# Layer 1's moves, a mixing, the last values, a plan and the short blocks take other places in the order of a two-layer attention kernel

## The chip, the core and the metric

The kernel runs on one core of a Trainium2 chip. The core has TensorE (PE: matrix products into the eight banks of PSUM), VectorE (DVE), ScalarE (ACT), GpSimd (POOL) and SyncE (SP), which here issues DMAs. The engines run at the same time. Each works through its own list of instructions in order, and they wait for one another through semaphores. The metric is the time of one execution on the device in microseconds (us); a change is judged by the median of several executions.

## What is computed

The input has 8 images of 256 channels and 32 x 32 = 1024 positions, all in 32-bit floats. Layer 0 is attention with 8 heads of 64. Layer 1 is attention with one head of 256 on normed tokens, then a mixture of 8 experts, 2 for each token:

```python
# layer 0: 8 heads, softmax over the queries (axis 1)
qkv = (xt @ w_qkv + b_qkv).reshape(B, S, N_HEADS, 3 * D_K)
attn = softmax(einsum('bihd,bjhd->bijh', q, k) * SCALE, axis=1)
x = einsum('bijh,bjhd->bihd', attn, v) @ w_out + b_out + xt
# layer 1: attention and experts, each on normed tokens, each added to t
n = layer_norm(t); scores = (n @ W.T) @ n.T
t = t + softmax(scores) @ n
n = layer_norm(t)
probs = softmax(n @ router_w.T); rw, re = top_k(probs, 2); rw = rw / rw.sum()
out = n
for e in range(8):
    h = gelu(n @ w1[e] + b1[e])
    out = out + combine[:, e:e + 1] * (h @ w2[e] + b2[e])
t = t + out
```

## The kernel before

**Order.** The kernel is written as a straight program. A planner sorts the instructions of each engine: it goes by the order in which they were written and by when its own model of costs says that their inputs are ready, so a later instruction that is ready passes an earlier one that is not. `tc.issue_after(x)` adds an edge: what is written inside comes after `x` on `x`'s own engine, and only there. Tiles have a fixed number of buffers; an instruction that writes one waits until its last reader is done. In PSUM there are three tiles of two banks ("big") and two of one bank ("acc"). A 32-bit product of 512 columns stands in the trace as two instructions.

**Images.** Images 0 to 6 run layer 0 (`layer0`), layer 1's attention (`attend`), the norm (`normed`) and the routing (`dispatch`), which scatters each token's row to the place of its expert in memory. Image 7 runs its layer 0, then the experts of the 7 other images (`experts`), then its own attention, and then the experts of its own tokens densely (`dense`), while the other images' results are added up and stored.

**Layer 0.** For each of 4 pairs of heads (g) there are 8 steps (j). Step `at` makes scores for the two heads (L531, two halves of 512 queries each), their maxima in two halves (L546, L555), the exps (L572), and, two steps later, the product with the values (`po`, L608). The values are divided by the exps' sums first (`vs`, L588). Eight blocks of values are projected ahead of the step that needs them: six during the image before, and the last two by `begun.rest()` after step 0 (L414, with additions L436 on DVE). The pairs' queries and keys are projected at the steps in `PROJECT`: (0, 3), (1, 1) and (2, 1) (`pqk`, L384); at the first of these the routing of the image before goes on, with two small products in a free bank (L1141) and a copy of them (L1147). At the last of these, DVE transposes the image into tokens (`residual`, L483), and in the two steps after it POOL adds the output's bias (L490). After 32 steps the heads are projected out (`pr`, L716). Between `po`'s two parts stand empty instructions on SP (`relay`, L618).

**The plan.** In image 7, `plan` computes which block of tokens belongs to which expert: a first part on DVE at step (1, 1), a second at (2, 1), before `residual` there. The last six small operations of the second part make three tables of addresses (L1310, L1313).

**Layer 1's attention.** Scores are made by a scheme with 7 products in place of 8, for four pairs of token blocks (`Pair`). `open` copies the first product (L797, ACT), starts the z product in an acc bank (L819) and adds (L829, DVE); `middle` makes a second copy (L808); `end` a third (L814); `rest` finishes, with the maxima and exps (L857 to L875). Each block's exps are then turned: a DVE transpose (L896) and 16 moves of 32 x 256, 8 by ACT and 8 by SP's DMAs (L908). `mix` multiplies them with the tokens (`py`, L925, an acc bank) and adds the result to the tokens on DVE (L934), which frees the bank. The order of these calls is written out by hand at the end of `attend`.

**Experts.** The rows of the 7 images are cut into 63 blocks: 56 full ones of 256 tokens and 7 short ones of 128, in an order that `Group` sets. For each block ACT copies the expert's weights into a ring (L1366), SP fetches rows (L1382), DVE transposes them (L1395), PE makes two layers of products (L1406, L1435), ACT the gelu (L1418), DVE adds the bias and multiplies by the gate (L1445, L1459), and POOL scatters the rows by indirect DMAs (L1466). The last 4 blocks (`LATE`) finish during image 7's attention.

**Dense.** For image 7, POOL adds the normed tokens (L1120) after the transposes of `normed`; DVE computes the gates (L1020 to L1606). Then, for each expert and half, PE makes `pdh` (L1630) and `pdy` (L1654), ACT the gelu (L1639) and DVE the weighted sum (L1664). At the third of the 16 rounds `biases` transposes the gates (L1612), copies them (L1614, ACT), multiplies them with the biases (`pb`, L1618) and adds (L1621).

Of the kernel before, what the change touches and what calls it, by code (L numbers as in the profile page):

```python
# [19 lines left out]
def kernel(  # L20
# [23 lines left out]
    nc = tc.nc  # L44
    P = 128
# [5 lines left out]
    NCC = C // P  # L51
# [443 lines left out]
    def layer0(b, xT, begun, routing, xs):  # L495
# [148 lines left out]
        for at in range(last + LAG + 1):  # L644
# [15 lines left out]
            if at <= last:  # L660

                with tc.issue_after(seconds[1].ins) if 1 in seconds else nullcontext():
                    first_max(at, 0)
                score(at, 0, 1)
                score(at, 1, 0)
                second_max(at, 0)
                if not early:
                    soften(at, 0)
                with tc.issue_after(seconds[0].ins):
                    ahead = divide(at - 1) if at > 0 else seconds[0]  # L670
                    if parts and at > 0:
                        parts.pop(0)(ahead)
                with tc.issue_after(ahead.ins):
                    first_max(at, 1)
            elif at == last + 1:
                evicted["divided"] = divide(last)
            if at == 0:
                score(0, 1, 1)
                second_max(0, 1)
                soften(0, 1)  # L680
                begun.rest()
                share()
# [5 lines left out]
            if at <= last and (g, j) in PROJECT:  # L688
                with tc.issue_after(firsts[at, 1].ins), tc.issue_after(array.ins):
                    share(firsts[at, 1])  # L690
                    pair, pq, mm = project_pair(b, xT, g + 1)
                qks.append(pair)
                if (g, j) == PROJECT[-1]:
                    ahead = firsts[at, 1]
                    if b == B - 1:
                        with tc.issue_after(ahead.ins):
                            ahead = next(planning)
                    with tc.issue_after(ahead.ins):
                        t1, parts = residual(b, xs)
                if g == 0:  # L700
                    with tc.issue_after(mm.ins), tc.issue_after(firsts[at, 1].ins):
                        counted = share(pq)
                if b == B - 1 and (g, j) == PROJECT[1]:
                    planning = plan(groups[0])
                    with tc.issue_after(firsts[at, 1].ins):
                        next(planning)
            elif at <= last and (g, j) > PROJECT[1]:
                share(firsts[at, 1])
        for _ in routing:
            pass  # L710
# [12 lines left out]
    def attend(b, t1, fill, tick=nothing, n1=None):  # L723
# [54 lines left out]
        class Pair:  # L778
# [17 lines left out]
            def open(self):  # L796
                self.first = nc.scalar.copy(self.left, self.x)  # L797
                if self.k < 3:
                    second = self.product(self.v, a12, b21, True)
                    tc.declare_no_dep(second.ins, self.first.ins, reason="the other bank")  # L800
                self.z = acc(f"ps1z_{b}_{self.k}")
                self.product(self.z, s1_, t1_, True)
                self.add(self.left, self.v, 3.0e38, self.low[0])
# [116 lines left out]
        def mix(at, aT, ssum, more):  # L920
# [16 lines left out]
            tick(("mixed", at), mixed)  # L937

# [23 lines left out]
        third = turned(*third, (pairs[2].first, pairs[2].second))  # L962
        fourth = turned(*fourth, (pairs[2].second, pairs[2].second))
        mix(*second)
        fifth, sixth = pairs[2].rest()
        pairs[3].open()
# [91 lines left out]
    class Group:  # L1058


        def __init__(self, n, items):
# [5 lines left out]
            halves = [(2 * j + 1) * self.nb // (2 * self.half) for j in range(self.half)]  # L1067
# [29 lines left out]
    def normed(b, t2, fill, tick=nothing, norm=None):  # L1097
# [16 lines left out]
        else:  # L1114
            with tc.issue_after(copied.ins):
                fill("turned")
            for part, at in ((n2.first, slice(0, NT - 1)), (n2.last, slice(NT - 1, NT))):
                for cc in range(NCC):
                    some = t2[:, at].rearrange("p i (k cc c) -> p cc i k c", k=NQ, c=SQ)[:, cc]
                    added = nc.gpsimd.tensor_add(  # L1120
                        some, some, part[:, :, ts(cc, P)].rearrange("p i (k c) -> p i k c", c=SQ)
                    )
                    tc.add_manual_dep(added.ins, evicted["scaled"].ins.name, BEHIND)
# [88 lines left out]
    def plan(group):  # L1212
# [94 lines left out]
        placed = nc.vector.tensor_copy(row_at[:, :nb], lo)  # L1307
        where = [row_at]
        for what, each in (("w", WE), ("b1", NFC), ("b2", D)):
# [4 lines left out]
            where.append(at)  # L1314
        group.where = where
        yield placed
# [271 lines left out]
    def dense(b, t2, norm, fill, begin, table):  # L1588
# [3 lines left out]
        _, nT, l = normed(b, t2, fill, norm=norm)  # L1592
# [13 lines left out]
        nc.vector.tensor_add(all_gates, all_gates, second)  # L1606

        def biases():

            pg = big(f"pg_{b}")  # L1610
            for i in range(NT):
                nc.tensor.transpose(pg[:E, ts(i, P)], all_gates[:, i, :], ident)  # L1612
            gT = two.tile([E, S], F32, tag="tr", name=f"gT_{b}")
            nc.scalar.copy(gT, pg[:E, :])  # L1614
            for i in range(0, NT, 2):
                pb = acc(f"pb_{b}_{i}")
                for j in range(2):
                    nc.tensor.matmul(  # L1618
                        pb[:, ts(j, D)], gT[:, ts(i + j, P)], b2_rows, start=True, stop=True
                    )  # L1620
# [63 lines left out]
        for at, (e, n) in enumerate((e, n) for e in range(E) for n in range(NH2)):  # L1684
            hT, mm = hidden(e, n, collected)
            if at == 2:
                biases()
            if pending is not None:
                collected = collect(*pending, mm)
            pending = e, n, hT  # L1690
# [106 lines left out]
```

## Time and profile before

| what | us |
|---|---|
| median of 3 runs (2270.83 to 2273.49) | 2272.08 |
| the profiled execution, its own time | 2274.83 |
| its span, first to last instruction | 2273.1 |
| busy of TensorE's weight loads (beside the products) | 1200.3 |
| scores of layer 0 (L531), busy | 566.0 |
| values product of layer 0 (L608), busy | 568.5 |
| exps of layer 0 (L572), busy on ACT | 570.4 |
| layer 0 of an image, first scores to the first output product (image 6: 1461.1 to 1602.7) | 141.6 |
| the same for image 7 (1700.2 to 1848.0) | 147.8 |
| experts of 7 images (1862.0 to 2062.4) | 200.4 |

In lists of the trace a line gives the start and the length in us, the engine, the line of the kernel, the operation, the tiles (what is written, an arrow, what is read), the shape and how many were merged. In brackets stands how long the engine had been idle before, and what ended that. "PEld" are weight loads, "SPq" is SyncE's queue. In tables by window the first entries are the stretch and its length, then for each engine its busy time and count, then the granted clock of TensorE (1.00 is full), the DMA engines' busy share and GB/s. Granted clock over the whole run: 0.996.

### The profile page before, as it was taken

What the parts mean: (1) busy time and instruction counts of PE and PEld (TensorE: products, weight loads), DVE (VectorE), ACT (ScalarE), POOL (GpSimd) and SP (SyncE); (2) the same over time, 40 slices, a digit from 0 to 9 for tenths busy, and PEclk for the clock granted to TensorE, in tenths of its full rate; (3) what the DMA queues carried; (4) which work ended last, traced back from release to release, by engine and by line L of the source; (5) the groups of instructions that cost most, each with busy time, mean ns of one, the idle gap of its engine ahead of it and who ended that gap; (6) DMA issues with size and microseconds to landing.
All of it is one profiled execution on the core that took longest, in us unless ns stands there. A gap on an engine that the chain in (4) does not pass through costs nothing.

```text
span 2273.1 us, 38013 instructions
## 1 busy us (share of the span) xinstructions
PE 2231.4 (98%) x13033; PEld 1200.3 (53%) x13033; DVE 1567.1 (69%) x3924; ACT 1231.3 (54%) x2221; POOL 309.7 (14%) x327
## 2 busy tenths in 40 slices
PE   9999999999999999999999999999999999999998
PEld 3345534563356335543555345534563368885666
DVE  5775678567865787577756775678557857665667
ACT  3664566356636564746554664566355655555411
POOL 1000012000300030002000120002000315551100
PEclk9999999999999999999999999999999999999999
DMA  8996201020102010111011010200032036662485
GB/s 279 357 352 199 53 15 43 3 61 7 51 1 46 19 51 7 31 35 43 15 19 46 20 38 10 55 13 27 1 78 64 31 70 148 149 148 48 120 276 169
DMA packets 273449, 181.89 MB, mean 80 GB/s; under 512 B 191860, under 2 KB 228519, under 8 KB 272232
## 3 DMA queue, kind: packets, MB, share of 16 engines
q1 hardware_dynamic: 260328, 149.16, 24.3%
q0 software_dynamic: 11296, 29.78, 3.6%
q8 instruction: 104, 1.70, 0.3%
q14 instruction: 89, 0.73, 0.1%
q10 hardware_dynamic: 1632, 0.52, 0.1%
HBM read 62.55 MB, written 105.70 MB: 74 GB/s over the span
## 4 chain that ended last, share of the span: by engine, by line
PE 80%; issue 5%; ACT 4%; DVE 4%; SPq 2%; POOL 2%; DMA 1%; POOLq 0%; DVEq 0%; ACTq 0%
PE po L608 20%; PE psc L531 20%; PE pqk L384 7%; PE py L925 7%; PE pr L716 5%; PE pv L414 4%; PE ps L819 3%; PE px L756 2%; POOL y L1466 2%; SPq L908 2%; PE pdh L1630 2%; PE pdy L1654 2%; PE pqk L362 2%; PE ps1z L819 2%; PE ph L1406 1%
## 5 line engine op out<-in xcount | busy, mean ns | idle before, releaser
L572 ACT ACTIVATE ex<-psc,nmax 128x1024 f32<-128x1024 f32 x512 | 570.4, 1115 | 298.8 <-DVE scrap L555 215.6
L608 PE MATMUL po<-ex,vs 64*64 64x512 f32 x4096 | 568.5, 592 | 5.3 <-DVE vs L588 4.3
L531 PE MATMUL psc<-qk,qk 64*64 64x512 f32 x4096 | 566.0, 593 | 3.7 <-ACT ex L572 3.6
L555 DVE TENSOR_SCALAR_CACHE_REDUCE scrap<-psc,nmax 128x512 f32<-128x512 f32 x512 | 384.5, 751 | 158.5 <-PE psc L531 129.8
L546 DVE TENSOR_REDUCE nmax<-psc 128x1 f32<-128x512 f32 x512 | 350.8, 685 | 10.7 <-PE psc L531 10.7
L531 PEld LDWEIGHTS psc<-qk,qk 64*64 64x64 f32 x4096 | 178.0, 132 | 275.1 <-ACT ex L572 129.0
L608 PEld LDWEIGHTS po<-ex,vs 64*64 64x64 f32 x4096 | 172.9, 132 | 284.0 <-DVE vs L588 87.6
L1203 POOL DMA_INDIRECT rows<-n,d_at x112 | 109.2, 975 | 463.4 <-DVE nmax L546 425.1
L384 PE MATMUL pqk<-xT,wqkv 128*128 128x512 f32 x384 | 171.2, 599 | 0.0
L1466 POOL DMA_INDIRECT y<-yb,to x119 | 117.4, 986 | 209.2 <-DVE yb L1459 185.6
L349 ACT ACTIVATE qk<-pqk,b_qks 128x512 f32<-128x512 f32 x124 | 85.6, 690 | 88.8 <-PE pqk L384 79.7
L384 PEld LDWEIGHTS pqk<-xT,wqkv 128*128 128x128 f32 x384 | 71.0, 190 | 99.9 <-issue 77.3
L908 ACT COPY spare<-home 32x256 f32<-32x256 f32 x272 | 109.4, 402 | 17.3 <-DVE home L896 11.9
L414 PE MATMUL pv<-wqkv,xT 128*128 128x512 f32 x244 | 116.4, 600 | 1.0 <-DVE v L436 1.0
L925 PE MATMUL py<-n,spare 128*128 128x256 f32 x512 | 114.9, 379 | 0.0
L1195 POOL IOTA n<- 128x8 f32 x14 | 2.0, 145 | 820.5 <-PE py L925 820.5
L1406 PE MATMUL ph<-xb,w_ring 128*128 128x256 f32 (+1 forms) x488 | 110.7, 370 | 2.9 <-DVE xb L1395 2.8
L716 PE MATMUL pr<-wo,res 128*128 128x256 f32 x512 | 111.9, 379 | 0.7 <-ACT res L627 0.7
L925 PEld LDWEIGHTS py<-n,spare 128*128 128x128 f32 x512 | 96.4, 190 | 20.1 <-issue 4.3
L716 PEld LDWEIGHTS pr<-wo,res 128*128 128x128 f32 x512 | 97.2, 190 | 17.8 <-ACT res L627 4.7
L1418 ACT ACTIVATE hb<-ph,b1T 128x256 f32<-128x256 f32 (+1 forms) x126 | 51.3, 459 | 101.1 <-PE ph L1406 101.1
L1435 PE MATMUL pe<-w_ring,hb 128*128 128x256 f32 x444 | 105.5, 379 | 0.0
(265 smaller groups left out, 2836.8 us busy)
## 6 DMA issues: line engine op xcount, KB each, us to landing
rows<-zero SPq DMA_DIRECT2D x7, 8256.0 KB, 62.4
xr<-rows SPq DMA_DIRECT2D x224, 64.0 KB, 2.0
xs<-in_x_dram SPq DMA_DIRECT2D x64, 128.0 KB, 3.9
ys<-y SPq DMA_DIRECT2D x16, 512.0 KB, 6.4
spare<-home SPq DMA_DIRECT2D x240, 32.0 KB, 1.9
out_dram<-oT SPq DMA_DIRECT2D x58, 128.0 KB, 3.8
xT<-in_x_dram SPq DMA_DIRECT2D x7, 1024.0 KB
sums<-t SPq DMA_DIRECT2D x7, 1024.0 KB
```

The lines of the kernel that those rows point to most:

```text
L384: mm = nc.tensor.matmul(pq[:, ts(n, 512)], wqkv[:, cc, t, ts(g, P)], xT[:, cc, ts(n, 512)], start=(cc == 0), stop=(cc == NCC - 1),)
L414: return nc.tensor.matmul(pv, self.xT[:, cc, ts(i, P)], wqkv[:, cc, 2, :], start=(cc == 0), stop=(cc == NCC - 1),)
L531: mm = nc.tensor.matmul(pss[at, h][ts(c, DK), ts(n, 512)], k[r, j * P + c * DK : j * P + (c + 1) * DK], q[r, ts(n, 512)], start=True, stop ...
L546: firsts[at, h] = nc.vector.tensor_reduce(nmax, pss[at, h][:, ts(0, 512)], AX.X, ALU.max, negate=True)
L555: seconds[h] = nc.vector.tensor_scalar(scrap, pss[at, h][:, ts(1, 512)], -1.0, nmaxes[at, h], ALU.mult, ALU.min, accum_out=nmax,)
L572: nc.scalar.activation(ex, pss.pop((at, h)), AF.Exp, bias=nmaxes.pop((at, h)), scale=1.0, accum_out=sums[at][:, h : h + 1],)
L608: mm = nc.tensor.matmul(po[n][ts(h, DK), :], vss[at][keys, h, :], exps[at, h][keys, ts(n, 512)], start=(j == 0 and turn == 0), stop=(j == ...
L716: nc.tensor.matmul(pr[:, :C], res[g][:, ts(i, P)], wo[:, g, :], start=(g == 0), stop=(g == NPAIR - 1))
L908: move(to[ts(k, SQ), a], since[ts(a, SQ), k])
L925: evicted["mixed"] = nc.tensor.matmul(py[:, :D], aT[m], n1[:, m, :], start=(m == 0), stop=(m == NT - 1))
L1406: last = nc.tensor.matmul(ph[:, ts(fc, br)], wb[:, dc * FF + fc * P : dc * FF + (fc + 1) * P], xb[:, dc, :], start=(dc == 0), stop=(dc == ...
L1466: sent = nc.gpsimd.indirect_dma_start(out=group.ways[sum(group.size[:b]) // P + r][:, :], out_offset=bass.IndirectOffsetOnAxis(ap=to[:, r ...
```

## The change

Seven places change:

- `begun.rest()` moves from the end of step 0 into step 1, between the scores of the first head and those of the second.
- In image 7, `residual` moves from step (2, 1) to step (0, 3), behind the first maximum of the second head there. In the other images it stays.
- `plan` stops after the first of its four tables, and again after each of the other three; these are computed in the steps after (2, 1).
- In `attend`, all ACT moves of the third block's turn are issued after the third pair's second copy; half of them were issued after its first copy only.
- `mix` returns its addition (L934), and the fourth pair's first addition is issued after that of the second mixing.
- The 7 short blocks go to places 4, 12, 20, ... 52, from 4, 13, 22, ... 58.
- In `dense` the normed tokens are added by DVE, after the gates, and no longer by POOL; the gates' transposes and their copy stay in the third round, behind its `pdh`; the bias products go to the fourth round, behind its `pdy`.

```diff
                 score(at, 0, 1)
+                if at == 1:
+                    begun.rest()
                 score(at, 1, 0)
...
                 soften(0, 1)
-                begun.rest()
                 share()
...
-                if (g, j) == PROJECT[-1]:
-                    ahead = firsts[at, 1]
-                    if b == B - 1:
-                        with tc.issue_after(ahead.ins):
-                            ahead = next(planning)
-                    with tc.issue_after(ahead.ins):
-                        t1, parts = residual(b, xs)
+                if (g, j) == PROJECT[-1] and b == B - 1:
+                    with tc.issue_after(firsts[at, 1].ins):
+                        next(planning)
                 if g == 0:
                     with tc.issue_after(mm.ins), tc.issue_after(firsts[at, 1].ins):
                         counted = share(pq)
+                if (g, j) == PROJECT[0 if b == B - 1 else -1]:
+                    with tc.issue_after(firsts[at, 1].ins):
+                        t1, parts = residual(b, xs)
...
             elif at <= last and (g, j) > PROJECT[1]:
                 share(firsts[at, 1])
+                if b == B - 1 and (g, j) > PROJECT[-1]:
+                    with tc.issue_after(firsts[at, 1].ins):
+                        next(planning, None)
...
-            def open(self):
+            def open(self, behind=None):
...
-                self.add(self.left, self.v, 3.0e38, self.low[0])
+                with tc.issue_after(behind.ins) if behind else nullcontext():
+                    self.add(self.left, self.v, 3.0e38, self.low[0])
...
-        third = turned(*third, (pairs[2].first, pairs[2].second))
+        third = turned(*third, (pairs[2].second, pairs[2].second))
         fourth = turned(*fourth, (pairs[2].second, pairs[2].second))
-        mix(*second)
+        mixed = mix(*second)
         fifth, sixth = pairs[2].rest()
-        pairs[3].open()
+        pairs[3].open(mixed)
...
-            halves = [(2 * j + 1) * self.nb // (2 * self.half) for j in range(self.half)]
+            each = (self.nb - LATE) // self.half
+            halves = [each // 2 + each * j for j in range(self.half)]
...
-                    added = nc.gpsimd.tensor_add(
-                        some, some, part[:, :, ts(cc, P)].rearrange("p i (k c) -> p i k c", c=SQ)
-                    )
-                    tc.add_manual_dep(added.ins, evicted["scaled"].ins.name, BEHIND)
...
         placed = nc.vector.tensor_copy(row_at[:, :nb], lo)
+        yield
         where = [row_at]
         for what, each in (("w", WE), ("b1", NFC), ("b2", D)):
...
             where.append(at)
+            yield
         group.where = where
-        yield placed
...
-        nc.vector.tensor_add(all_gates, all_gates, second)
+        gated = nc.vector.tensor_add(all_gates, all_gates, second)
+        for part, at in ((n2.first, slice(0, NT - 1)), (n2.last, slice(NT - 1, NT))):
+            for cc in range(NCC):
+                some = t2[:, at].rearrange("p i (k cc c) -> p cc i k c", k=NQ, c=SQ)[:, cc]
+                with tc.issue_after(gated.ins):
+                    gated = nc.vector.tensor_add(
+                        some, some, part[:, :, ts(cc, P)].rearrange("p i (k c) -> p i k c", c=SQ)
+                    )
...
             if at == 2:
-                biases()
+                gT = biases(mm)
             if pending is not None:
                 collected = collect(*pending, mm)
+            if at == 3:
+                bias_products(gT, collected)
```

## The prediction

> **What bounds the kernel now.** I read the page's busy shares first, then the waits of TensorE, then the timeline and the windows around each wait. TensorE is the engine to watch:
>
> ```profile
> PE 2231.4 (98%) x13033; PEld 1200.3 (53%) x13033; DVE 1567.1 (69%) x3924; ACT 1231.3 (54%) x2221; POOL 309.7 (14%) x327
> ```
>
> Only some 42 us are left in which PE does nothing, so the change can win little more than these gaps and what follows them. The table of PE's waits says what they are (total us, times, longest):
>
> ```profile
> PE ps1z L819 <- DVE t L934: 8.4, 8, 1.1
> PE ps L819 <- ACT home L808: 5.6, 7, 0.8
> PE po L608 <- DVE vs L588: 4.3, 9, 0.7
> PE psc L531 <- ACT ex L572: 3.6, 2, 2.8
> PE ph L1406 <- DVE xb L1395: 2.8, 2, 2.5
> PE pb L1618 <- ACT gT L1614: 1.4, 1, 1.4
> ```
>
> Two come once in nearly every image, in layer 1's attention. The timeline of image 6 shows both (start, length, engine, line; in brackets the idle time before and its releaser):
>
> ```profile
> 1652.91 1.65 ACT L908 COPY spare<-home 32x256 f32<-32x256 f32 x4 [1.31 <-DVE home L896]
> 1654.58 0.59 ACT L808 COPY home<-ps 128x512 f32<-128x512 f32 x1
> 1655.21 1.13 PE L819 MATMUL ps<-mixes,xa 128*128 128x512 f32 x2 [0.79 <-ACT home L808]
> ...
> 1661.43 0.69 DVE L829 CUSTOM_DVE_ANT_0 home<-home,ps 128x512 f32<-128x512 f32 x1 [2.02 <-ACT home L797]
> 1662.04 0.48 DVE L934 SCALAR_TENSOR_TENSOR t<-py,rs,t 128x256 f32<-128x256 f32 x1
> 1662.58 1.13 PE L819 MATMUL ps1z<-mixes 128*128 128x512 f32 x2 [1.06 <-DVE t L934]
> ```
>
> ACT makes four moves (L908) before the third pair's second copy (L808), for which PE waits; its source was ready from 1652.70, where PE's product ended. Later DVE sits 2.02 us on the fourth pair's first addition, which waits for a copy, while the mixing (L934) behind it has long had its sums; PE needs that mixing, since it frees the bank for the fourth pair's z product.
>
> **Third pair's moves behind the copy.** The four moves are not removed but change places with L808. ACT is idle at 1651.6 to 1652.9, so L808 starts at about 1652.74 instead of 1654.58, and PE, whose work before ends at 1654.4, no longer waits. Worth per image: the 0.79 shown, plus a tail of 0.16 (a 512-column product is written as 0.59, but the next starts 0.43 after it), plus 0.10 for a slower first product after a gap: 1.05. Seven times: 7.4. The SyncE moves of the same call are not on ACT's queue and keep their times; the ACT moves end as before, since the sum of work ahead of the last is the same. Cover: the third mixing needs the moves by 1662.2 then, and the last of its eight DMAs is issued at 1657.50 and takes 1.9 to land, so 2.8 us stand.
>
> **First addition behind the mixing.** The mixing then runs at 1659.9 instead of 1662.04. PE, ready at 1661.35 by its cadence, began at 1662.58, plus 0.10 slow start: 1.3 each, 8 times, 10.6. What waits behind on DVE: the addition itself starts no earlier than its copy allows (1661.43), so the even half's addition and the exp at 1663.22 move by only 0.5 to 0.7. That exp stands ahead of the fourth pair's second copy on ACT (1665.73), which PE needs after the third mixing: old slack 1.6 us, new about none. I take 0.25 per image back for it: 7.4 + 10.6 - 2.0 = 16.0. Bounds: 5.3 (ACT's chain alone sets the pace, 8 x 0.66) and 18.
>
> **Last values a step later.** Eight products (3.43 us) and two additions (0.69 each) move from behind step 0's scores to the middle of step 1. Gone: the wait of po on vs, 0.41 shown, 0.57 by cadence. Paid: scores of the two heads use different 64-row halves and run side by side, 8 in 0.86; with the values put between them, the 8 of head 0 in step 1 go alone, 1.72. Old stretch in image 6, 1461.05 to 1469.99: 8.94. New: 1.75 (step 0) + 0.22 (two small transposes) + 1.72 + 3.43 + 1.72 = 8.84, and a slow start or two. I take 0 for it; bounds +4.6 (8 x 0.57) and -6.5 (8 x 0.81).
>
> **Residual and plan, last image.** At the third projection DVE works through the plan's second part and then two transposes, and the scores' maxima come late:
>
> ```profile
> 1789.64 2.37 DVE L483 STREAM_TRANSPOSE t<-xs 128x1024 f32<-128x1024 f32 x2
> 1794.01 1.99 PE L531 MATMUL psc<-qk,qk 64*64 64x512 f32 x8 [2.81 <-ACT ex L572]
> ```
> ```profile
> 1791.20:1794.00 2.80, 0.01 (x1) 0.00 (x0) 2.68 (x5) 1.21 (x2) 0.00 (x0) 1.00 0.00 0
> 1794.00:1797.40 3.40, 3.39 (x16) 1.05 (x20) 2.45 (x8) 1.69 (x3) 2.62 (x2) 0.50 0.02 5
> ```
>
> In these windows the number after the engines' entries is the granted clock: after the gap PE runs 3.4 us at half speed. Lost: 2.81 + 0.16, and the first eight scores and eight po in 1.99 and 1.85 instead of 1.09 and 1.04: 4.7. Taken away from DVE: 2.37 (transposes) and 1.35 (six small operations, 1788.29 to 1789.64). DVE is then done at 1788.3, and the first maximum is wanted 1.16 after the scores begin at 1787.54, at 1788.7. The gain is the 4.7. The transposes go to the first projection, where DVE idles 5.40 us (1720.06 to 1725.46) with PE busy on projections; their source landed long before, their target is free once the stored sums left (issued at 1699.51, 4.7 to land elsewhere). If the count's copy gets ahead of them there, 2.4 us and a slow window, some -4, come back. The two POOL additions of 2.37 follow in steps 4 and 5, where POOL has nothing else. The six small operations come back in three steps at 0.45 each, and a step leaves DVE about 0.19 idle: -0.3. Together 4.4; bounds -4 and 4.7.
>
> **Half blocks.** Of 63 blocks of tokens the short ones move from 4, 13, ... 49, 58 to 4, 12, ... 44, 52, so that ten full ones end the run. The one real gap of that stage follows block 58:
>
> ```profile
> 2057.26 0.69 DVE L1445 TENSOR_TENSOR yb<-pe,b_all 128x512 f32<-128x512 f32 x1 [3.49 <-DMA y<-yb,to]
> 2059.44 2.98 PE L1406 MATMUL ph<-xb,w_ring 128*128 128x256 f32 x8 [2.55 <-DVE xb L1395]
> ```
>
> DVE waits for a buffer whose rows POOL sent late, and PE for the transpose behind it. Price: 2.55 + 0.16, then eight products in 2.98 instead of 1.89 and 16 transposes in 2.62 instead of 1.92: 4.5, and 0.2 of the gap at 1906.37. The short block at 2021.87 has the same wait on DVE, 1.52, and PE does not stop. I take 3.5; bounds 4.7 and -4.5, one more such gap.
>
> **Dense tail.** POOL's four additions hold up DVE's gates, and later PE waits for ACT and then runs slowly:
>
> ```profile
> 2148.66 4.14 POOL L1120 TENSOR_TENSOR t<-t,n 128x896 f32<-128x896 f32 x2
> 2148.84 4.47 DVE L1033 TENSOR_TENSOR g_p<-g_p,g_z 128x64 f32<-128x64 f32 x1
> 2161.58 6.18 PE L1618 MATMUL pb<-b_rows,gT 8*128 8x256 f32 x16 [1.42 <-ACT gT L1614]
> ```
> ```profile
> 2161.58:2164.60 3.02, 3.02 (x10) 2.41 (x11) 1.64 (x3) 0.00 (x0) 0.00 (x0) 0.68 1.01 414
> 2164.60:2167.70 3.10, 3.10 (x9) 1.96 (x7) 1.17 (x2) 0.00 (x0) 0.00 (x0) 0.50 1.06 369
> 2167.70:2171.00 3.30, 3.30 (x9) 2.67 (x9) 0.69 (x1) 0.00 (x0) 0.00 (x0) 0.50 0.99 389
> ```
>
> On DVE the same additions cost 1.10 twice (between the rows 128x512 at 0.69 and 128x1024 at 1.24) and 0.29 twice, 2.8, against 4.2 of blocking removed; they end at about 2155.4, when the first experts' sums arrive, so nothing is paid. The bias transposes keep their place, and the products come a step later, when gT is long there. From 2160.0 to 2173.8 PE did 16 bias products and 16 of the experts, 6.9 at full clock: 6.9 is the ceiling. Against it: the bias sums' additions stand behind the totals and their transpose on DVE (2.47 + 1.25), and PE has two banks for them; if it waits, -3.7.
>
> The clock is the other unknown. It fell after 1.42 idle and stayed at 0.50 through 6 us of unbroken bias products on 8 rows, while after the 2.81 gap above it came back in 3.4. Read so, the products themselves hold it down, about 1.7 to 3.4 lost again; I take 4.5, bounds -3.7 and 6.9.
>
> The Trainium skill ("TensorE: Matmul & The Clock Gate", Part 1) has the clock halve after an idle window of about 3.4 us and return after a busy one. By that rule a gapless tail keeps full clock and the whole 6.9 comes; the rows here, which fell after a shorter gap and stayed down while PE was busy, speak against it.
>
> **Sum.** 16.0 + 0 + 4.4 + 3.5 + 4.5 = 28.4. The profiled execution took 2274.8 (span 2273.1 and 1.7 around it), so it would take 2246.4; the median of the runs is 2.7 lower, 2272.1, and 2272.1 - 28.4 = 2243.7, said as 2244.
>
> **Rivals.**
> - *ACT's chain takes the place of the waits in the attention* (0.18): the 16.0 becomes 5.3. For it: the exp moves by only 0.66 where PE moves by 2.3. Against: 1.6 us of slack ahead of that copy. 28.4 - 10.7 = 17.7: 2254.
> - *The change does not do what it says* (0.08): the order on each queue is set by a planner from its own costs, and an edge forced in one place may let another late instruction pass; then the attention keeps its two waits and only plan, half blocks and tail count, 12.4, or 8.9 without the blocks: 2260 to 2263. Against: both edits are edges on the very engine that is late.
> - *Slower through the values* (0.07): their two additions stand in DVE's queue ahead of step 1's maxima and wait for PE; the exps then come late, score buffers too, and PE gets a gap like that at 1794, 2.81 plus half clock, 4.7 in each image. 8 x 4.7 = 37.6 against 28.4: 2281. It decides from 28.4 / 8 = 3.6 us per image; against it, DVE idles about 1 us in that stretch and PE has other scores to do.
>
> **How the numbers follow.** The forecast, 2244, has 0.62, its own range 2235 to 2253. A measurement of this kernel tells about 0.2%, 4.5 us, from nothing. Faster: 0.62 + 0.18 + 0.08 = 0.88; slower 0.07; 0.05 for gains and losses that meet within 4.5. Range: from all ceilings together (18 + 4.6 + 4.7 + 4.7 + 6.9 = 38.9, 2233.2) to 2262, past the first rival and into the second.
>
> **What would show it.** After: the rows ps1z <- t and ps <- home gone from PE's waits, and images 2.0 us apart less than the 239 of before; no psc gap of 2.8 in the last image and 62.7 instead of 67.4 from its third projection to pr; no ph gap above 1; DVE's L1033 at 0.2; the bias products without a wait, and their clock, which settles the 4.5. The forecast is wrong if PE's waits only change their names (a copy L808 of the fourth pair, or moves landing late), or if the first four steps of an image grow beyond 15.3 us.

## The result and the profile after

| | us |
|---|---|
| before, median of 6 runs | 2270.60 |
| after, median of 6 runs (2251.71 to 2261.46) | 2256.48 |
| ratio, with its 95% interval | 0.9937 [0.9918, 0.9955] |
| forecast | 2244 (2233 to 2262) |

The kernel became 14.1 us faster, half of the 28.4 that were forecast. The six runs fall into two groups: three at a granted clock of 0.999 took 2251.7 to 2253.7, three at 0.996 to 0.997 took 2259.3 to 2261.5. The profiled one, 2260.28 (span 2258.5), is of the second group. The clock turns out to be part of the change's effect, so both groups count.

To see where the time went I took the start on PE of the same instruction in both traces at the ends of seven stretches that together hold all of the difference. `px` (L756 before, L759 after) are the products of tokens and W that begin layer 1's attention; the mixings are the eight groups of `py`.

| stretch | before | after | difference | forecast |
|---|---|---|---|---|
| first four steps, 8 images | 124.59 | 126.46 | +1.87 | 0 |
| `px` to the fourth mixing, images 0 to 6 | 320.95 | 309.90 | -11.05 | -16.0 with image 7 |
| `px` to the eighth mixing, image 7 | 68.96 | 68.42 | -0.54 | (in the 16.0) |
| fourth to eighth mixing, images 0 to 6 | 121.12 | 122.79 | +1.67 | 0 |
| third projection to `pr`, image 7 | 67.48 | 62.94 | -4.54 | -4.4 |
| experts, `pr` to `px` of image 7 | 217.41 | 214.21 | -3.20 | -3.5 |
| eighth mixing of image 7 to the end | 138.78 | 139.97 | +1.19 | -4.5 |
| sum (spans: 2273.1 and 2258.5) | | | -14.6 | -28.4 |

The page's busy shares and PE's waits after the change (us in total, times, longest):

```profile
PE 2236.2 (99%) x13033; PEld 1205.7 (53%) x13033; DVE 1564.7 (69%) x3928; ACT 1228.1 (54%) x2221; POOL 304.7 (13%) x323
```
```profile
PE ps L823 <- DVE nlow L833: 3.9, 7, 0.6
...
PE ph L1406 <- DVE xb L1395: 1.3, 2, 1.1
...
PE ps1z L823 <- DVE nlow L833: 1.0, 1, 1.0
...
PE po L608 <- DVE vs L588: 0.7, 1, 0.7
...
PE psc L531 <- ACT ex L572: 0.4, 1, 0.4
```

Every wait that was to go has gone: no `ps1z <- t`, no `ps <- home`, no score wait of 2.8, no wait of `pb`. One row is new, `ps <- nlow`, 0.56 in each of images 0 to 6. PE is busy 4.8 us longer than before with the same 13033 instructions. That is not the clock: over the whole run PE spent less time at half clock than before (13.65 us against 17.06, leaving out the last microseconds). It stems from the images' first four steps, where PE is busy 125.97 in place of 120.16; e3 below shows why. The timeline of image 6 shows the new wait:

```profile
1650.28 3.74 ACT L912 COPY spare<-home 32x256 f32<-32x256 f32 x9
...
1652.31 0.48 DVE L938 SCALAR_TENSOR_TENSOR t<-py,rs,t 128x256 f32<-128x256 f32 x1 [1.33 <-PE py L929]
...
1653.83 1.02 PE L823 MATMUL ps1z<-mixes 128*128 128x512 f32 x2
...
1654.04 0.58 ACT L800 COPY home<-ps 128x512 f32<-128x512 f32 x1
...
1654.66 0.69 DVE L833 CUSTOM_DVE_ANT_0 home<-home,ps 128x512 f32<-128x512 f32 x1 [1.86 <-ACT home L800]
...
1655.41 1.13 PE L823 MATMUL ps<-mixes 128*128 128x512 f32 x2 [0.56 <-DVE nlow L833]
```

The mixing (L938) now runs as soon as its sums are there, and the z product at 1653.83 has no wait. But the fourth pair's middle product (1655.41) now waits for the first addition (1654.66), and that one for the copy L800, which stands on ACT behind nine moves.

In the tail the windows (after the engines' entries: granted clock, DMA share, GB/s) and the timeline of PE show this:

```profile
2156.70:2160.00 3.30, 3.30 (x8) 1.37 (x8) 3.30 (x5) 0.00 (x0) 0.00 (x0) 0.69 1.08 327
2160.00:2163.50 3.50, 3.50 (x6) 1.36 (x5) 0.92 (x2) 0.00 (x0) 0.00 (x0) 0.50 0.94 333
2163.50:2167.00 3.50, 3.50 (x7) 1.94 (x7) 0.69 (x1) 0.00 (x0) 0.00 (x0) 0.50 0.90 283
2167.00:2170.00 3.00, 3.00 (x7) 2.04 (x7) 0.00 (x0) 1.26 (x2) 0.00 (x0) 0.50 0.64 257
```
```profile
2154.63 1.13 PE L1631 MATMUL pb<-b_rows,gT 8*128 8x256 f32 x4
2155.69 1.12 PE L1643 MATMUL pdh<-n2T,table 128*128 128x512 f32 x2
...
2159.70 2.07 PE L1631 MATMUL pb<-b_rows,gT 8*128 8x256 f32 x4
2161.70 2.08 PE L1643 MATMUL pdh<-n2T,table 128*128 128x512 f32 x2
```

PE is busy all the time, with no gap in the 8 us ahead, and still its clock is at half from 2157.9 on, for 13.65 us by the record of the clock (10.24 at this place before). At half clock that is a loss of about 6.8 (half of 13.65), and the middles of the two groups of runs lie 7.6 us apart. So in a run without the fall this stretch would be an estimated 133.1 us long, 5.6 shorter than before and not 1.2 longer. The planner also dealt the bias products out in fours between the products of the next expert.

### The profile page after: what moved, and what is told of

The parts are those of the page before. It is cut to its first block, busy times and chain, and to the rows that moved or that the text cites. A ratio compares the mean times of both kernels' runs of the same rounds, so it can differ in the third digit from the quotient of the medians.

```text
span 2258.5 us, 38012 instructions
## 1 busy us (share of the span) xinstructions
PE 2236.2 (99%) x13033; PEld 1205.7 (53%) x13033; DVE 1564.7 (69%) x3928; ACT 1228.1 (54%) x2221; POOL 304.7 (13%) x323
## 4 chain that ended last, share of the span: by engine, by line
PE 84%; issue 7%; ACT 3%; DVE 3%; POOL 3%; DMA 1%; DVEq 0%; POOLq 0%; SPq 0%; ACTq 0%
PE psc L531 20%; PE po L608 19%; PE py L929 8%; PE pqk L384 8%; PE ps L823 5%; PE pr L719 4%; PE pv L414 4%; PE pdh L1643 3%; POOL y L1466 2%; PE px L759 2%; PE pdy L1667 2%; PE pqk L362 2%; ACT spare L912 2%; PE ps1z L823 2%; PE ph L1406 1%
## 5 line engine op out<-in xcount | busy, mean ns | idle before, releaser
L608 PE MATMUL po<-ex,vs 64*64 64x512 f32 x4096 | 581.1, 591 | 1.7 <-DVE vs L588 0.7
L531 PE MATMUL psc<-qk,qk 64*64 64x512 f32 x4096 | 582.0, 592 | 0.5 <-ACT ex L572 0.4
L531 PEld LDWEIGHTS psc<-qk,qk 64*64 64x64 f32 x4096 | 182.7, 132 | 274.6 <-ACT ex L572 126.4
L608 PEld LDWEIGHTS po<-ex,vs 64*64 64x64 f32 x4096 | 179.7, 132 | 273.0 <-issue 84.5
```

Source lines behind the costliest of these rows:

```text
L531: mm = nc.tensor.matmul(pss[at, h][ts(c, DK), ts(n, 512)], k[r, j * P + c * DK : j * P + (c + 1) * DK], q[r, ts(n, 512)], start=True, stop ...
L608: mm = nc.tensor.matmul(po[n][ts(h, DK), :], vss[at][keys, h, :], exps[at, h][keys, ts(n, 512)], start=(j == 0 and turn == 0), stop=(j == ...
```

## The experiments

Times are medians; each ratio is against runs of the kernel before on the same chip, whose median is given. The runs f1, e5, e6 and b_all shared a chip on which the kernel before took 2275.40 and, in each of their profiles, image 0's second mixing came 2.0 to 2.8 us later, so they are compared by ratio and by stretches.

**The bias products over 128 rows** (e1_rows128).

```diff
-        b2_rows = two.tile([E, D], F32, tag="hb", name="b2_rows")
-        nc.sync.dma_start(b2_rows, b2)
+        b2_rows = two.tile([P, D], F32, tag="hb", name="b2_rows")
+        nc.gpsimd.memset(b2_rows, 0.0)
+        nc.sync.dma_start(b2_rows[:E, :], b2)
...
-            gT = two.tile([E, S], F32, tag="tr", name=f"gT_{b}")
-            nc.scalar.copy(gT, pg[:E, :])
+            gT = two.tile([P, S], F32, tag="tr", name=f"gT_{b}")
+            nc.gpsimd.memset(gT, 0.0)
+            nc.scalar.copy(gT[:E, :], pg[:E, :])
```

> The changed kernel with its bias products over 128 rows: the table of biases and the transposed gates are set to zero over all 128 partitions (two POOL memsets) and the same 32 products of 256 columns take K=128, so their number and length on PE stay; the result is the same. Theory (products on 8 rows hold the granted clock down, whether or not PE idles): the 0.50 windows at 2157 to 2171 go, span clock 0.999 in every run, the stretch from the last px to the end falls from 208.4 to about 201.5 and the time is 2252 or a little less in every run, no second cluster at 2260. Rival (the clock falls for another reason, such as what DMA or the other engines do then, or all of the tail being on PE without a gap): the 0.50 windows stay, runs between 2252 and 2261 as before.

Measured: 2251.36 (2250.99 to 2254.06), before 2272.16, ratio 0.9909 [0.9894, 0.9923], all four runs at 0.998 or 0.999. From the eighth mixing to the end: 133.49 instead of 139.97. The windows over the same products:

```profile
2156.30:2159.80 3.50, 3.50 (x14) 2.32 (x13) 3.24 (x5) 0.00 (x0) 0.00 (x0) 1.00 1.05 250
2159.80:2163.20 3.40, 3.40 (x13) 2.28 (x12) 3.40 (x5) 0.00 (x0) 0.00 (x0) 1.00 0.82 304
```

The clock stays at 1.00, with the order on PE unchanged, DVE busier and the DMA engines about as busy. The second group of runs is gone. The other runs agree: of those with the changed dense part on 8 rows (after, e2, e3, e5) 12 of 23 had a clock of 0.997 or less, of those on 128 rows (e1, b_all, b4) none of 12; b2 and b3 are left out, since their clock fell in layer 0.

**The same in the kernel before** (f1_before_rows128), where PE waits 1.42 ahead of these products: the same edit, made there.

> The kernel before, with nothing changed but the bias products over 128 rows in place of 8 (zeros below; two POOL memsets more). PE's wait of 1.42 for the transposed gates ahead of them stays. Theory (the rows hold the clock down, the wait has no part in it): no 0.50 window from 2160 to 2175, the stretch from the last px to the end falls from 207.7 to about 202.6, and the time is 5 less, 2267. Rival (the wait starts the fall): a window of 3.41 at 0.50 is left behind the wait, 1.7 of the 5 stay lost, 2269.

Measured: 2272.47, before 2275.40, ratio 0.9983 [0.9975, 0.9992], which is 3.9 us. Its timeline and window:

```profile
2165.72 3.90 PE L1620 MATMUL pb<-b_rows,gT 128*128 128x256 f32 x16 [1.42 <-ACT gT L1616]
```
```profile
2165.70:2169.50 3.80, 3.78 (x16) 2.79 (x16) 2.06 (x3) 0.00 (x0) 0.00 (x0) 1.00 0.95 274
```

The wait of 1.42 is there to the hundredth, the 16 instructions take 3.90 in place of 6.18, and the clock is 1.00. The times can't choose between theory and rival: the interval of the ratio is 1.8 to 5.7 us, and they expected about 5 and 3.3. Nor can one profile, since with 8 rows the run e5 below had no fall at this place either. All profiles together can. Of the seven with 8 rows six have half clock over these products: 13.65 us (after, e3), 10.24 (before, f2) and 6.83 (e2, e4), in after, e2 and e3 with no gap on PE in the 8 us ahead. Of the six with 128 rows (e1, f1, b_all, b2, b3, b4) none has (e6 has 32 rows, and is told of below). So it is the rows, and no wait is needed.

In this profile the stretch from the last `px` to the end took 206.7, not the 202.6 of the theory. Two things ahead of the bias products cost it time. The clock fell for 3.41 at 2145.45, and a subtraction of DVE, late by it, took 3.90 beside POOL's four additions (L1120, 2149.08 to 2154.01). The exp behind it was late, and PE waited for a gelu:

```profile
2149.80 3.90 DVE L1027 TENSOR_TENSOR g_p<-g_l,g_m 128x64 f32<-128x64 f32 x1
...
2153.73 0.26 ACT L1028 ACTIVATE g_p<-g_p 128x64 f32<-128x64 f32 x1 [4.93 <-DVE g_p L1027]
...
2156.12 3.87 PE L1656 MATMUL pdy<-table,dh 128*128 128x256 f32 x16 [1.73 <-ACT dh L1641]
```

In the profile of the kernel before, the same additions stood beside a multiplication behind that exp (L1033, 4.47), and PE did not wait. So the old dense part can cost another 1.7, where the clock falls just ahead of it (f1, e4), and the change took this away together with POOL's additions. The edit's own work on POOL, setting `gT` to zero, was done by 2117.8.

**Bias products over 32 rows** (e6_rows32): the same edit with `SQ` (32) in place of `P`.

> The changed kernel with bias products over 32 rows in place of 8 (24 of zeros). Theory (the part of the array's rows that works counts, and a quarter is still little): 0.50 windows as with 8 rows, times between 2252 and 2261. Rival (only the very few rows of 8 fall below what counts): full clock and 2251 to 2252 in every run, as with 128 rows.

Measured: 2258.08, before 2275.40, ratio 0.9928 [0.9915, 0.9940]. No window at half clock over the products. But the run e5 below, with 8 rows on the same chip, had none in its profile either, so whether 32 rows are enough stays open. Both show a second cost of few rows at full clock. In e5:

```profile
2159.70 1.12 PE L1631 MATMUL pb<-b_rows,gT 8*128 8x256 f32 x4
2160.76 1.12 PE L1643 MATMUL pdh<-n2T,table 128*128 128x512 f32 x2
2161.81 1.13 PE L1631 MATMUL pb<-b_rows,gT 8*128 8x256 f32 x4
```

A round of four and two takes 2.11 (2159.70 to 2161.81), with 32 rows 2.11 too, and 1.72 with 128: four rounds, 1.6 us. From the eighth mixing to the end e5 took 134.99, with the same dense part that took 139.97 in the profile after; its one window of 3.41 at half clock in this stretch lies at 2131.67, ahead of the products.

**The dense part as it was** (e4_olddense): POOL's additions back behind the transposes, transposes and bias products back in the third round.

> The changed kernel with the whole dense part as it was (four additions on POOL, transposes and bias products at once, all in one place). Theory (the dense part is worth nothing when the clock falls and about 6 when it does not): time between that of the changed kernel's slower runs and 3 above its mean, about 2257 to 2260, every run with the 0.50 windows near the bias products, so no two clusters or smaller ones. Rival (the dense part is worth the 4.5 that was forecast in every run): 2261, 4.5 above the changed kernel's median.

Measured: 2258.92 (2257.15 to 2260.86), before 2272.16, ratio 0.9940 [0.9927, 0.9953]; from the eighth mixing to the end 141.06. The times are as the theory had them: over groups with and without a fall, the dense part as changed is worth nothing that these runs can tell. The profile has the late subtraction of f1 too (L1032 here, 3.93, after a fall at 2127.38) and a wait of 1.8 for a gelu behind it, which the profile before doesn't have.

**The middle product free of the first addition** (e2_nodep).

```diff
                     mm = self.product(self.x, s2_, t2_, False)
+                tc.declare_no_dep(mm.ins, self.opened.ins, reason="the other bank")
```

> The changed kernel in which a pair's middle product no longer waits for the pair's first addition, which reads the other bank. Theory (half of the gain of the addition behind the mixing was given back to this new wait): the row ps <- nlow of 3.9 us in PE's waits goes, the stretch from the second to the third mixing in images 0 to 6 goes from 7.72 to 7.1 to 7.3, 3 to 4.5 us in all. Rival (ACT's chain is the bound behind it: the copies L800 and L812 and the exp keep their times): PE waits as long for the pair's second copy L812 instead, the stretch to the fourth mixing keeps its sum, and the time is that of the changed kernel within 1 us.

Measured: 2258.16, before 2272.16, ratio 0.9938 [0.9926, 0.9950]. Second to third mixing 7.42 instead of 7.72, of which the next mixing gives back 0.10: a gain of 1.3 in seven images, not 3 to 4.5. The wait moved on:

```profile
1652.36 0.58 ACT L800 COPY home<-ps 128x512 f32<-128x512 f32 x1
...
1652.98 0.69 DVE L834 CUSTOM_DVE_ANT_0 home<-home,ps 128x512 f32<-128x512 f32 x1 [1.86 <-ACT home L800]
...
1654.40 0.92 PE L930 MATMUL py<-n,spare 128*128 128x256 f32 x3 [0.28 <-DVE nmax L834]
```

The third mixing needs the bank that the even half's maximum frees, and on DVE that maximum stands behind the first addition, which waits for the copy. The rival held in the main: a copy on ACT sets the pace here. But the wait is not for the second copy (L812) that it named; it goes back to the first (L800).

**The addition's place undone** (e5_addition_undone), `pairs[3].open()` in place of `pairs[3].open(mixed)`, **and the addition's place alone** in the kernel before (f2_addition_alone).

> The changed kernel with the fourth pair's first addition where it was, ahead of the second mixing on DVE. Theory (the edit brought only 0.5 an image, and 1.2 in the last): the second to third mixing takes 8.2 again, 7 x 0.5 + 1.2 - 0.7 = 4 more, 2257 in a run at clock 0.999, 2264 in one at 0.997. Rival (the edit is worth the 8.6 that was forecast and hid a loss elsewhere): 2261 and 2268.

> The kernel before, with nothing changed but the fourth pair's first addition behind the second mixing on DVE. Theory (the mixing no longer holds PE up, but the pair's middle product waits for the late addition, and that for ACT's copy, whose place behind the moves is unchanged): the second to third mixing takes 7.6 to 7.8 instead of 8.2, the row ps1z <- t of 8.4 goes and a row ps <- nlow of about 4 comes, 3 to 5 us in all with the last image's 1.2. Rival (what was forecast): 6.9 to 7.2, 8.6 in all.

Both of my theories missed. Undone: ratio 0.9933 [0.9917, 0.9950] (2257.97, before 2275.40), second to third mixing 7.74 against 7.72. The order on DVE did not even change back:

```profile
1655.33 0.48 DVE L938 SCALAR_TENSOR_TENSOR t<-py,rs,t 128x256 f32<-128x256 f32 x1 [1.32 <-PE py L929]
1657.70 0.69 DVE L833 CUSTOM_DVE_ANT_0 home<-home,ps 128x512 f32<-128x512 f32 x1 [1.89 <-ACT home L800]
```

Once nine moves stand ahead of the copy, the planner puts the mixing first by itself; the edge is redundant. So no run has the moves with the old order on DVE. Alone in the kernel before, the edge is worth nearly what was forecast: 2265.52, before 2272.73, ratio 0.9965 [0.9952, 0.9977], 8.0 us; second to third mixing 6.97 in place of 8.22. In its image 6:

```profile
1654.35 0.59 ACT L797 COPY home<-ps 128x512 f32<-128x512 f32 x1
...
1654.97 0.69 DVE L830 CUSTOM_DVE_ANT_0 home<-home,ps 128x512 f32<-128x512 f32 x1 [1.11 <-ACT home L797]
...
1655.75 1.10 PE L820 MATMUL ps<-mixes 128*128 128x512 f32 x2
...
1656.68 3.62 PE L926 MATMUL py<-n,spare 128*128 128x256 f32 x16
```

Now the four kernels side by side, in us after `px` in image 6: ACT's first copy of the fourth pair, and the third mixing.

| | copy | third mixing | between |
|---|---|---|---|
| before | 37.08 | 40.67 | 3.59 |
| addition alone (f2) | 37.09 | 39.42 | 2.33 |
| moves without the edge (e5) | 36.80 | 39.12 | 2.32 |
| both (after) | 36.76 | 39.09 | 2.33 |

In the last three the mixing follows the copy by the same 2.33: copy 0.6, addition 0.7, the middle product 1.0. Either edit alone brings PE up to the copy, and the second finds nothing left.

**The last values back in step 0** (e3_values).

```diff
                 score(at, 0, 1)
-                if at == 1:
-                    begun.rest()
                 score(at, 1, 0)
...
                 soften(0, 1)
+                begun.rest()
                 share()
```

> The changed kernel with layer 1's last value products back in step 0. Theory (their place between the scores splits up scores of the two heads that else run side by side): the first four steps of an image go back from 15.63 to about 15.3, 7 x 0.33 = 2.3 us less, although the wait of 0.41 for the divided values comes back. Rival (the 0.3 came from the planner's other choices, not from this move): 15.6 stays.

Measured: 2254.18, before 2272.16, ratio 0.9921 [0.9908, 0.9933]. First four steps in 8 images 124.58, against 126.46 after and 124.59 before: the move costs 1.9 us, though the wait of 0.41 is back. After the change the stretch looks like this in image 6:

```profile
1456.58 1.93 PE L531 MATMUL psc<-qk,qk 64*64 64x512 f32 x8
1458.45 3.70 PE L414 MATMUL pv<-wqkv,xT 128*128 128x512 f32 x8
1462.08 1.50 PE L531 MATMUL psc<-qk,qk 64*64 64x512 f32 x10
1463.00 0.60 PE L608 MATMUL po<-ex,vs 64*64 64x512 f32 x2
1463.42 0.60 PE L531 MATMUL psc<-qk,qk 64*64 64x512 f32 x2
```

The first head's eight scores run alone, and behind the values `psc` and `po` alternate in twos and fours, where in the kernel before they come in eights.

**Four edits together** (b_all): e1, e2, e3, and ACT's first copy of the fourth pair ahead of the fourth block's moves. In it that copy overwrites the fourth block's exps before they are turned, so its output is not the reference's; the order and the number of instructions are as meant.

> The changed kernel with four edits together: bias products over 128 rows; last values back in step 0; middle product not waiting for the first addition; and ACT's first copy of the fourth pair put ahead of the fourth block's eight moves. Theory (in the run without the wait on the other bank PE waited instead 0.28 for the even half's maximum, which stood on DVE behind the first addition, and that one waited for a copy that stood on ACT behind nine moves): with the copy ahead, the stretch from the second to the third mixing goes from 7.42 to 7.0 to 7.1 in images 0 to 6 with no wait of PE on nlow or nmax; with 0.33 x 6 for the values and 6.5 for the clock the time is 2245 to 2247, every run. Rival (ACT is full: what the copy gains the moves lose, and a later mixing waits for moves): the stretches after the third mixing grow by 0.3 to 0.6 and the time is 2248 to 2250.

Measured: 2252.45, before 2275.40, ratio 0.9901 [0.9887, 0.9916]. Second to third mixing 6.89, without a wait; third to fourth 5.40 in place of 5.17 in images 1 to 6, and fourth to eighth 126.01 in all in place of the 122.79 after. The theory held for the stretch and the rival for the later mixings and the time: at this ratio a kernel before of 2272.1 gives 2249.6, inside the rival's 2248 to 2250.

**The same with the copy behind the turn's transpose, and the values in a third place** (b2_together, b3_seventh): the values stand in step 1 behind both heads' scores. b3 also gives the seventh block four moves on SP in place of six.

```diff
             nc.vector.transpose(sq, ex)
+            if callable(behind):
+                with tc.issue_after(pairs[2].third.ins):
+                    behind = (behind(),) * 2
...
-        fourth = turned(*fourth, (pairs[2].second, pairs[2].second))
+        fourth = turned(*fourth, pairs[3].early)
...
                 score(at, 1, 0)
+                if at == 1:
+                    begun.rest()
...
-                    away = (a + k) % 2 and (i < 6 or a > 0)
+                    away = (a + k) % 2 and (i < 6 or a > 1)
```

> The changed kernel with bias products over 128 rows, the last values in step 1 behind both heads' scores (not between them), the middle product not waiting for the first addition, and ACT's first copy of the fourth pair ahead of the fourth block's moves. Theory: second to third mixing 6.9 in images 1 to 6, tail at clock 1.00 in 202, the first four steps 15.1 to 15.3: 2244 to 2247 on a chip where the kernel before takes 2271. Rival (moves land late behind the copy): the mixings after the third grow by 0.3 to 0.6 each image, 2248 to 2250.

> The same as the run b2_together, with four of the seventh block's sixteen moves on SyncE in place of six. Theory (the seventh mixing waits for the last of six DMAs, each 0.61 to issue and one in some images 1.4): the sixth to seventh mixing takes 3.46 to 3.5 in every image instead of 3.5 to 4.4, 2 to 3 us less in all than b2_together. Rival (ACT's two more moves end later than the DMAs did, and the square root's table behind them too): same or up to 2 more.

Measured: 2266.96 and 2268.24, before 2272.73, ratios 0.9974 [0.9961, 0.9987] and 0.9979 [0.9968, 0.9991]; clock 0.992 to 0.995. In the attention the theories held: second to third mixing 6.89, and the sixth to the seventh 3.45 or 3.46 in images 0 to 6 of b3 (3.45 to 3.66 in b2, 3.46 to 3.86 after). The seventh block's moves brought 0.8 against b2 from the fourth mixing to the eighth, not the 2 to 3 expected, since b2 had little of that wait left. But the first four steps took 153.95 and 150.65 in all, against 126.46. In image 1 of b2:

```profile
265.82 1.93 PE L531 MATMUL psc<-qk,qk 64*64 64x512 f32 x8
268.92 1.73 PE L531 MATMUL psc<-qk,qk 64*64 64x512 f32 x4 [1.17 <-ACT ex L572]
270.59 6.39 PE L414 MATMUL pv<-wqkv,xT 128*128 128x512 f32 x8
```
```profile
266.37 1.28 ACT L572 ACT_TABLE_LOAD   x1 [2.30 <-DVE scrap L555]
...
274.41 0.69 DVE L436 TENSOR_TENSOR v<-pv,b_v 128x512 f32<-128x512 f32 x1 [3.02 <-PE pv L414]
```
```profile
268.90:272.40 3.50, 3.48 (x6) 1.03 (x7) 1.91 (x6) 2.31 (x5) 0.00 (x0) 0.54 0.00 0
272.40:276.00 3.60, 3.60 (x6) 1.48 (x5) 0.69 (x1) 0.00 (x0) 0.00 (x0) 0.50 0.00 0
```

PE runs ahead into the second head's scores and waits 1.17 for a score buffer, which the image's first exp frees late, behind a table load of 1.28 on ACT. With the values in step 0 PE has them to do meanwhile. The clock halves over the scores and the eight values that follow (6.39 in place of 3.70).

**The best of them** (b4_best): b3 with the values in step 0.

> The run b3_seventh with the last values back in step 0. Theory (the values between the two steps' scores starved PE: a wait for a score buffer of 1.0 to 1.5 and then 3.4 to 6.8 at half clock in each image): the first four steps go from 15.8 to 22.5 back to 15.0 to 15.6, 17.5 in the last image, 26 in all, and nothing else changes: 2241 to 2243 on a chip where the kernel before takes 2272, clock 0.998 to 0.999 in every run. Rival (half of what the two runs with this place lost has another cause): 2248 or more.

Measured: 2244.07 (2242.08 to 2245.87), before 2272.23, ratio 0.9876 [0.9860, 0.9893]: faster than both kernels, and just above the 2241 to 2243 expected. First four steps 124.53, `px` to the fourth mixing in images 0 to 6 304.16, fourth to eighth 120.82, the tail 133.46. In image 6:

```profile
1642.50 0.58 ACT L799 COPY home<-ps 128x512 f32<-128x512 f32 x1
...
1643.11 3.32 ACT L920 COPY spare<-home 32x256 f32<-32x256 f32 x8
...
1646.48 1.02 PE L828 MATMUL ps<-mixes 128*128 128x512 f32 x2
...
1647.34 2.97 PE L937 MATMUL py<-n,spare 128*128 128x256 f32 x13
```

The copy now starts 4.84 ahead of the third mixing, eight moves follow it, and PE has no wait. The third mixing comes 38.28 after `px`, 2.4 earlier than before: what both edits had promised together (1.05 and 1.3) is there once the copy is out of the way and the middle product no longer waits for the addition.

## Why the prediction was half right

- **Third's moves, 7.4.** `px` to the second mixing: 32.46 to 31.39, 1.07 seven times, 7.5. Right.
- **First addition, 10.6, less 2.0 for both.** The edit alone is worth its 1.3 an image (f2: 1.25), but the two do not add: 11.6 came in place of 16.0, 1.58 per image in place of 2.1 to 2.35. The step that failed is the sentence that the addition "starts no earlier than its copy allows" and then takes only the even half's addition and the exp along. PE's middle product also waits for it, and behind that the third mixing. Of the same copy the first part had said that ACT's work ahead stays the same; both edits therefore ended at one fixed point, and their gains had to be capped there, not summed. The slack of 1.6 that I priced was that of the pair's second copy. The rival "ACT's chain" named the right engine with too high a price (10.7 lost; 4.4 were).
- **Last values, 0.** It cost 1.9, inside the bounds (4.6 won to 6.5 lost). The 0.41 was won. Up to the first `po` the working held: 8.67 in image 6, against 8.84 in the working and 8.94 before, though with two scores fewer done. The loss lies behind that, where the working stopped: from there to the first projection 6.95 in place of 6.41, while `psc` and `po` alternate in twos and fours.
- **Residual and plan, 4.4, and half blocks, 3.5.** 4.54 and 3.20, and `psc` runs through where the gap was. Right for the residual, whose stretch is 67.48 to 67.51 in three profiles of the old order and 62.94 to 62.96 in all of the new. The experts are less sure: with the old order of blocks they took 217.41, 218.03 (f2) and 214.78 (f1), with the new one 212.65 to 214.85. The means differ by 2.7, but a single pair of profiles can show anything from 0 to 5, so that 3.20 came out so near to 3.5 is partly luck.
- **Dense, 4.5.** It was 1.2 lost in the profiled run, and by the estimate above 5.6 won in a run whose clock does not fall; the 4.5 came in neither group. The waits went as forecast (L1038 takes 0.22, `pb` waits for nothing). The clock term is what was mis-sized: "about 1.7 to 3.4 lost again" was 6.8, half of 13.65, and 1.6 more went into the changes between 8 and 128 rows (e1, whose tail has one window of 3.41 at half clock in another place, is 6.5 shorter in all). The mechanism, read from rows that stayed at 0.50 while PE was busy, is now shown by e1 and the count over all profiles. The Trainium skill ("TensorE: Matmul & The Clock Gate", Part 1) has the clock drop after an idle window; here it dropped in a stretch in which the profile has no idle time of PE at all, so the measurement decides against the rule for products on 8 rows.
- **Not in the sum: the seventh mixing.** Images 3 to 6 waited up to 0.4 for the seventh block's moves on SP, 1.7 in all. That moves landing late would be a way to fail was said, without a price.
- **Slower through the values** did not come in the place chosen; one place further (b2) its outcome appeared, a gap at the scores and then half clock, but not by the road that it told: PE waited before the values' products had begun, for the first exp, and not behind the two additions (L436), which ran later. The price was 3.3 to 3.7 us an image (153.95 and 150.65 against the 124.58 of e3, over 8) where 4.7 were named.

Of the signs named, several spoke against the forecast: the first four steps grew to 15.63 (15.3 was the limit), the images came 1.1 closer, not 2.0, a wait of PE changed its name (`nlow`, 3.9), and one gap of `ph` was 1.1, just above the limit of 1.

## What to carry to other kernels

When two edits remove two waits on the way to the same instruction, look for the thing both paths still need, here one copy on ACT, and cap the sum at what that thing allows. Here the two together moved the third mixing by 1.58, hardly more than the better one alone (1.55), and the whole 2.4 came only when the copy moved too. After a wait is taken away, follow what the released engine asks for next through every reader of the same tile; a dependency on the other bank counts. And products on few rows are not short work for PE: fill them up to full rows. Keeping the sixteen together did not spare the kernel before its 10.24 us at half clock.

## What the runs showed of the hardware

- Products on 8 rows let the clock fall while PE is busy without a gap. With the same instructions in the dense part the fall lasted 13.65 us (after), 6.83 (e2) and nothing (e5). All falls that end within a run last 3.41, 6.83, 10.24 or 13.65, multiples of 3.41. The Trainium skill ("TensorE: Matmul & The Clock Gate", Part 1) calls the window free-running; that would explain why identical code falls into two groups of times, but no run here moved the window's place by itself.
- The length of a gap alone does not decide: 1.42 us with no fall behind it (f1, 128 rows), and 1.17 followed by 6.83 at half clock (b2, scores on 64 rows). At the start of the tail, around the transposes of the norm, PE has the same two gaps of 0.87 and 1.21 among the same products in every profile; in 8 of the 14 a window of 3.41 at half clock followed, in 6 none. So something beside the instructions decides too. That few working rows are what the falls over the bias products and over the scores have in common is an inference for the scores; it is shown for the bias products alone. That the window's place alone made the difference there stays untested.
- A change between products on 8 or 32 rows and on 128 costs about 0.2 us (1.6 over eight changes) at full clock.
- A DVE operation on two inputs of 128x64 took 3.90 us (f1), 3.93 (e4) and 4.47 (before) beside POOL's additions of 128x896; the same rows take 0.2 otherwise.
